# LayerNorm of an image pair: rstd on VectorE and gamma on GpSimd for 17 tiles of each half

## The chip, the core and the metric

The kernel runs on one core of a Trainium2 chip. A core has five engines, each with an instruction queue of its own that it works through in order: TensorE (PE, with its weight loads as PEld), VectorE (DVE), ScalarE (ACT), GpSimd (POOL) and SyncE (SP), which here only issues DMAs. Engines wait for each other through semaphores. The metric is the device time of one execution in microseconds; the profile adds a trace of one execution, in which times are counted from the start of its span.

## The reference

Two layers, on 32 images of 128 channels and 56x56 pixels, all in float32. The first is a depthwise convolution, a LayerNorm over channels and a mixture of experts; the second a coordinate attention and a 3x3 convolution. The change lies in the LayerNorm and what hangs on it:

```python
x = conv_general_dilated(input, dw_kernel, (1, 1), ((3, 3), (3, 3)), feature_group_count=C) + dw_bias
x = transpose(x, (0, 2, 3, 1))
mu = x.mean(-1, keepdims=True)
var = x.var(-1, keepdims=True)
x = (x - mu) / sqrt(var + 1e-06) * ln_gamma + ln_beta
xf = x.reshape(T, C)                       # T = 32*56*56 = 100352 tokens
logits = xf @ Wg + bg                      # 8 experts
topv, topi = top_k(logits, 2)
wts = softmax(topv, axis=-1)
...
return input + x_skip + moe_out            # x_skip is the normalised x
```

## The kernel before

The program runs in stages, one after the other. (1) The depthwise convolution writes its result to DRAM (`y_d`), line 165 and what is around it. (2) The LayerNorm with the gates, lines 194 to 349: the stage of the change. (3) Routing and the experts, lines 352 and on. (4) The combination, attention and the second convolution, with its GpSimd transforms around lines 1022 to 1032.

Stage 2 goes over 16 pairs of images. A pair has 49 tiles of 128 tokens (`TPP`), taken as two halves, the `Unit`s, of 24 and 25 tiles. For each half:

- `centre`: a load of the pair (line 298, SP's queue); for each tile a product on TensorE with a matrix `proj` that subtracts the mean over the channels and gives the 8 logits beside it (line 310); ScalarE copies three tiles at a time to `cen` (line 311), and squares: in the first half tile by tile with a sum (line 315), in the second into `sqs` (line 317).
- `spread`: in the second half VectorE sums the squares (line 322). GpSimd makes the variance (line 323) and `rstd` by a power of -0.5 (line 324), for all tiles of the half in one instruction each.
- `normalise`: VectorE multiplies each tile of `cen` by `rstd` and gamma into the pair's row buffer `pair.row` (called `xn`), line 331, one instruction a tile; then the logits by `rstd` (line 333).

For each pair, `top` finds the two best experts (lines 237 to 252), ScalarE an exponential (line 255), and `gates` makes the weights, writes them into the last columns of the row buffer (lines 261 to 274) and issues the store of the row buffer to `acc_d` (line 276, SP's queue, 3356.5 KB). A row of `xn` has 137 numbers: 128 channels, 8 gates and a mark.

Buffers limit how far engines run ahead: four of `cen` (halves), two of `xn` (pairs), two of the loaded image pair, three of `rstd` and of `var` (halves), eight PSUM tiles of three token tiles each.

The order in which the instructions of each engine stand is settled when the program is built: the framework's scheduler places them by its own estimates of cost, so that instructions of one pair stand between those of another, and adds the semaphore waits. The engines keep to that order when the program runs.

Of the kernel before, what the change touches and what calls it, by code (L numbers as in the profile page):

```python
# [13 lines left out]
ALU = mybir.AluOpType  # L14
# [4 lines left out]
N, C, H, W = 32, 128, 56, 56  # L19
# [5 lines left out]
P = 128  # L25
# [17 lines left out]
def bc(ap, shape):  # L43
    return ap.to_broadcast(shape)
# [3 lines left out]
def moe_conv_then_coordatt_kernel(ctx: ExitStack, tc: tile.TileContext, a: dict, out: bass.AP):  # L48
    nc = tc.nc
# [14 lines left out]
    def load(name, shape, src, eng=None):  # L64
        t = const.tile(list(shape), F32, name=name)
        (eng or nc.sync).dma_start(t, src)
        return t
# [12 lines left out]
    gamma_bc = load("gamma_bc", [P, C], a["ln_gamma"].rearrange("c x -> x c").partition_broadcast(P))  # L80
# [113 lines left out]
    with ExitStack() as st:  # L194
# [6 lines left out]
        halves = ((0, TPP // 2), (TPP // 2, TPP))  # L201
        U = TPP - TPP // 2
        NSQ = TPP // 2
        rank_e = sp.tile([P, E], F32, name="rank_e", bufs=1)
        for e in range(E):
            nc.gpsimd.memset(rank_e[:, e : e + 1], float(E - e))
# [11 lines left out]
        def over_experts(x, n):  # L218
            return bc(x.unsqueeze(2), [P, n, E])
# [60 lines left out]
        class Unit:  # L280
# [12 lines left out]
            def centre(self):  # L293
# [8 lines left out]
                self.var = self.tile(sp, "var")  # L302
                self.alone = 0 if self.h else NSQ
                if self.alone < self.n:
# [21 lines left out]
            def normalise(self):  # L326
                pair = pairs[self.i]
                if self.h == 0:
                    pair.open()
                for j in range(self.n):  # L330
                    nc.vector.scalar_tensor_tensor(pair.row[:, self.j0 + j, 0:C], self.cen[:, j, 0:C],
                                                   self.rstd[:, j : j + 1], gamma_bc, ALU.mult, ALU.mult)
                nc.vector.tensor_tensor(pair.l[:, self.j0 : self.j1, :], self.cen[:, :, C : C + E],
                                        over_experts(self.rstd, self.n), ALU.mult)

        units = [Unit(i, h) for i in range(NPAIR) for h in range(2)]
        for k in range(len(units) + 3):

            pair = pairs[(k - 3) // 2] if k >= 3 else None
# [797 lines left out]
```

## Time and profile before

| what | us |
|---|---|
| median of 6 runs | 4894.09 |
| lowest and highest of the 6 | 4870.55, 4899.64 |
| the profiled execution | 4895.35 |
| its span | 4893.3 |
| stage 2 in it | 627 to 1095 |
| in these 468 us: PE, PEld busy | 364.1, 350.3 |
| DVE busy | 429.5 |
| ACT busy | 289.1 |
| POOL busy | 168.4 |

Over the whole span PE is busy for 74%, DVE 53%, POOL 56%, ACT 30%. The first number of a row of groups is the busy time of the group in us, the next the mean duration of one instruction in ns, and behind the bar stands the idle time of the engine before these instructions, with what ended it. Instructions of one engine overlap a little, so that the step from one to the next can be shorter than a duration.

In stage 2 the store of a pair is issued every 27.47 us (809.87, 837.33, 864.80) and the load of an image pair as often (791.32, 818.80, 846.27).

### The profile page before, as it was taken

How to read it: one execution, taken by the hardware profiler on the slowest of the kernel's cores; microseconds unless marked ns; L12 is line 12 of the kernel's file. 1: busy time of each engine (PE TensorE's matmuls, PEld its weight loads, DVE VectorE, ACT ScalarE, POOL GpSimd, SP SyncE). 2: the span in 40 equal slices, each digit the busy share in tenths (PEclk: the TensorE clock that was granted, in tenths of full speed). 3: DMA queues.
4: the chain of work that ended last, by engine and by line, in shares of the span. 5: the costliest groups of instructions: out<-in, count | busy, mean ns of one | idle time of the engine just before them, and what ended most of it. 6: DMA issues, size and time to landing. Idle time of an engine off the chain costs nothing. (4 is left out here: it accounts for less than half of the span.)

```text
span 4893.3 us, 60979 instructions
## 1 busy us (share of the span) xinstructions
PE 3630.5 (74%) x21765; PEld 2039.8 (42%) x21765; DVE 2585.5 (53%) x5562; ACT 1444.2 (30%) x3123; POOL 2738.3 (56%) x2044
## 2 busy tenths in 40 slices
PE   7998988841486486567557756677775998999999
PEld 4555488741243243233223323233332454545444
DVE  3333359996365267464521211111125888888787
ACT  0000066630232232223223323233341233333323
POOL 5444333331556654464555455655547878788875
PEclk9999998865687788778778977788887999999999
DMA  9999956539611211111111111111115555555552
GB/s 179 188 187 182 159 214 252 232 163 335 195 35 34 49 38 36 35 42 34 48 43 38 43 43 42 45 37 39 42 41 189 165 189 189 163 185 183 190 165 78
DMA packets 678003, 580.90 MB, mean 119 GB/s; under 512 B 405848, under 2 KB 611184, under 8 KB 667248
## 3 DMA queue, kind: packets, MB, share of 16 engines
q1 hardware_dynamic: 411408, 319.81, 22.8%
q10 hardware_dynamic: 222816, 160.70, 12.5%
q0 software_dynamic: 43264, 94.64, 7.2%
q8 instruction: 186, 3.05, 0.3%
q14 instruction: 329, 2.70, 0.2%
HBM read 314.92 MB, written 260.09 MB: 118 GB/s over the span
## 5 line engine op out<-in xcount | busy, mean ns | idle before, releaser
L703 POOL DMA_INDIRECT acc_d<-yo,row x676 | 703.1, 1040 | 756.2 <-issue 474.1
L662 PE MATMUL ph<-fxt,w 128*128 128x512 f32 (+1 forms) x1400 | 753.4, 674 | 401.2 <-ACT ht L663 364.9
L1042 PE MATMUL pc<-v,wk 128*128 128x392 f32 x1920 | 704.9, 509 | 0.4 <-POOL v L1027 0.4
L663 ACT ACTIVATE ht<-ph,bias 128x512 f32<-128x512 f32 (+1 forms) x700 | 473.1, 682 | 719.4 <-remote 334.2
L670 PE MATMUL py<-ht,w 128*128 128x512 f32 (+1 forms) x1400 | 658.8, 615 | 0.0
L641 POOL DMA_INDIRECT xg_r<-acc_d,idx x556 | 534.0, 960 | 197.5 <-issue 153.1
L165 PE MATMUL acc<-xs,band 28*64 28x432 f32 (+1 forms) x11264 | 538.2, 530 | 60.3 <-issue 39.2
L662 PEld LDWEIGHTS ph<-fxt,w 128*128 128x128 f32 x1400 | 276.7, 214 | 723.0 <-ACT ht L663 447.4
L1042 PEld LDWEIGHTS pc<-v,wk 128*128 128x128 f32 x1920 | 348.0, 191 | 308.9 <-issue 105.7
L165 PEld LDWEIGHTS acc<-xs,band 28*64 28x64 f32 x11264 | 308.7, 133 | 289.2 <-issue 184.7
L310 PE MATMUL lnps<-proj,lnyt 128*128 128x136 f32 x1568 | 364.1, 398 | 68.3 <-ACT sq L315 39.0
L670 PEld LDWEIGHTS py<-ht,w 128*128 128x128 f32 x1400 | 270.9, 202 | 287.8 <-issue 285.9
L310 PEld LDWEIGHTS lnps<-proj,lnyt 128*128 128x128 f32 x1568 | 350.3, 315 | 82.7 <-ACT sq L315 48.1
L654 DVE COPY fxt<-pt 128x512 f32<-128x512 f32 (+1 forms) x175 | 119.4, 683 | 439.4 <-remote 184.4
L1052 DVE SCALAR_TENSOR_TENSOR y<-pc,y 128x392 f32<-128x392 f32 x640 | 317.4, 553 | 13.8 <-PE pc L1042 13.8
L697 DVE TENSOR_TENSOR ys<-pb,xg_r 128x512 f32<-128x512 f32 (+2 forms) x147 | 98.4, 671 | 425.3 <-PE pb L679 245.6
L959 POOL TENSOR_TENSOR cxn<-cxn,cx 128x896 f32<-128x896 f32 x112 | 268.0, 2401 | 80.3 <-DMA cxn<-acc_d 34.7
L672 ACT ACTIVATE fyt<-py,b 128x512 f32<-128x512 f32 (+1 forms) x175 | 119.4, 682 | 650.3 <-PE py L670 471.9
L1022 POOL TENSOR_TENSOR d<-pad 128x3248 f32<-128x3248 f32 x32 | 228.0, 7126 | 147.7 <-DVE pad L1014 147.7
L181 DVE TENSOR_TENSOR yt<-acc,m 128x448 f32<-128x448 f32 x256 | 143.8, 619 | 268.0 <-PE acc L165 247.1
L448 PE MATMUL ps_r<-cnt_r,ones 128*128 128x1 f32 x400 | 85.1, 293 | 265.9 <-DVE junk L447 119.9
L641 POOL DMA_INDIRECT xg_f<-acc_d,idx x120 | 115.1, 959 | 225.8 <-DVE thr_r L460 90.1
(244 smaller groups left out, 5258.1 us busy)
## 6 DMA issues: line engine op xcount, KB each, us to landing
acc_d<-xn SPq DMA_DIRECT2D x16, 3356.5 KB
acc_d<-yo ACTq DMA_DIRECT2D x4, 13426.0 KB
lnyt<-y_d SPq DMA_DIRECT2D x16, 3136.0 KB
x<-in_x SPq DMA_DIRECT2D x16, 3136.0 KB
cxn<-acc_d SPq DMA_DIRECT2D x112, 448.0 KB
cx<-acc_d SPq DMA_DIRECT2D x112, 448.0 KB
out<-y ACTq DMA_DIRECT2D x64, 784.0 KB
xt<-in_x SPq DMA_DIRECT2D x64, 392.0 KB
```

The source lines that it names most:

```text
L165: nc.tensor.matmul(acc[r][half * M : (half + 1) * M, :, lo:hi], lhsT=band[rows, t0 + o - least, 1 - par : 1 - par + M], rhs=xs[i][rows, ha ...
L181: nc.vector.tensor_tensor(yts[r][:, :, i - 1 : W : 2], acc[r], common[r], ALU.add)
L310: nc.tensor.matmul(ps[:, j, :], lhsT=yf[:, self.j0 + g + j, :], rhs=proj, start=True, stop=True)
L641: d = nc.gpsimd.indirect_dma_start(out=xg[0:n, k, :], out_offset=None, in_=acc_d[0:T1, :], in_offset=bass.IndirectOffsetOnAxis(ap=idx[0][0 ...
L662: nc.tensor.matmul(ph[:, 0:N_], lhsT=w[0][:, f * P : (f + 1) * P], rhs=xt[:, 0:N_], start=True, stop=True)
L663: nc.scalar.activation(ht[:, f, 0:N_], ph[:, 0:N_], AF.Gelu, bias=w[2][:, f : f + 1])
L670: nc.tensor.matmul(py[:, 0:N_], lhsT=w2[:, f, :], rhs=ht[:, f, 0:N_], start=(f == 0), stop=(f == NF - 1))
L703: d = nc.gpsimd.indirect_dma_start(out=acc_d[:, :], out_offset=bass.IndirectOffsetOnAxis(ap=row[0:n, k : k + 1], axis=0), in_=yo[0:n, k, : ...
L959: nc.gpsimd.tensor_tensor(xn, xn, x2, ALU.add)
L1022: nc.gpsimd.tensor_tensor(d, high, low, ALU.subtract)
L1042: nc.tensor.matmul(m[k], lhsT=wk[k][:, dw, :], rhs=v[:, k, rows, dw : dw + W], start=(dw == 0), stop=(dw == 2))
L1052: nc.vector.scalar_tensor_tensor(r[x], m[k], f, r[y_], ALU.mult, ALU.add)
```

## The change

In `normalise`, 17 of the 24 or 25 tiles of a half are no longer taken one by one. One VectorE instruction multiplies the 17 tiles by `rstd`, spread over the channels, into the row buffer; one GpSimd instruction then multiplies these 17 tiles in the row buffer, in place, by gamma, spread over the tiles. The other 7 or 8 tiles stay as they were.

```diff
         NSQ = TPP // 2
+        NTWO = 17
...
                 if self.h == 0:
                     pair.open()
-                for j in range(self.n):
+                two = pair.row[:, self.j0 : self.j0 + NTWO, 0:C]
+                shape = [P, NTWO, C]
+                nc.vector.tensor_tensor(two, self.cen[:, 0:NTWO, 0:C], bc(self.rstd[:, 0:NTWO].unsqueeze(2), shape), ALU.mult)
+                nc.gpsimd.tensor_tensor(two, two, bc(gamma_bc.unsqueeze(1), shape), ALU.mult)
+                for j in range(NTWO, self.n):
                     nc.vector.scalar_tensor_tensor(pair.row[:, self.j0 + j, 0:C], self.cen[:, j, 0:C],
                                                    self.rstd[:, j : j + 1], gamma_bc, ALU.mult, ALU.mult)
```

`bc` spreads an operand to a shape without copying it. The store of a pair now waits for GpSimd as well as for VectorE. The scheduler places the instructions of stage 2 anew; in the built program the logits of both halves now stand ahead of the multiplications of the first, and both halves of a pair are multiplied close to each other.

## The prediction

> **What bounds the kernel now.** I read the busy time of each engine in stretches of the LayerNorm stage first, then the groups of that stage, then its order of time. The columns of the first view are the stretch in us from the span's start, its length, and for PE, PEld, DVE, ACT and POOL the busy us with the number of instructions; then the granted clock, the share of DMA and GB/s.
>
> ```profile
> 720.00:780.00 60.00, 51.63 (x222) 49.42 (x221) 59.32 (x164) 40.33 (x169) 21.84 (x10) 0.87 0.60 244
> 780.00:840.00 60.00, 51.49 (x217) 48.74 (x217) 59.32 (x171) 40.99 (x175) 25.95 (x9) 0.84 0.58 237
> 840.00:900.00 60.00, 51.53 (x219) 48.91 (x218) 59.28 (x173) 39.17 (x166) 23.88 (x10) 0.83 0.63 258
> ...
> ```
>
> VectorE is busy 59.3 of every 60 us: it sets the pace of this stage, which runs from 627 us to 1095 us. TensorE comes next, and its weight loads (one for each matmul) came back to back at 10.69 us for 48 from 818.85 on, so 98 of them, one pair of images, need about 21.8 us. A pair takes 27.47 us now (the tile reductions on line 322 start at 803.60 and 831.07). ScalarE works 18.5 us of that, GpSimd 11. The groups show what VectorE does and what GpSimd waits for:
>
> ```profile
> L331 DVE SCALAR_TENSOR_TENSOR xn<-cen,rstd,gamma_bc 128x128 f32<-128x128 f32 x784 | 213.9, 344 | 47.3 <-POOL rstd L324 47.3
> ...
> L324 POOL TENSOR_TENSOR rstd<-var,mhalf 128x24 f32<-128x24 f32 (+1 forms) x32 | 139.7, 4364 | 2.7
> ...
> L322 DVE TENSOR_REDUCE var<-sqs 128x25 f32<-128x3200 f32 x16 | 55.7, 3481 | 4.0 <-ACT sqs L317 4.0
> L323 POOL TENSOR_SCALAR var<-var 128x24 f32<-128x24 f32 (+1 forms) x32 | 26.4, 826 | 320.0 <-DVE var L322 169.9 <-ACT sq L315 149.9
> ```
>
> The change takes from the top line and gives to GpSimd, which is idle most of the stage. The question is whether the two engines can work at the same time on such operations. Two places in the order of time answer it, the first just behind the stage, the second in the last one (start, duration, engine, line):
>
> ```profile
> 1095.62 0.57 DVE L248 TENSOR_TENSOR oh<-rank_e,second 128x392 f32<-128x392 f32 x1
> 1095.65 2.88 POOL L723 TENSOR_TENSOR w<-w,ls_bc 128x512 f32<-128x512 f32 x2 [3.46 <-DMA w<-in_W]
> 1096.11 1.27 DVE L252 TENSOR_TENSOR later<-later,second 128x49 f32<-128x49 f32 x1
> 1097.30 1.30 DVE L262 TENSOR_TENSOR w<-m,one_t 128x49 f32<-128x49 f32 x1
> 1098.52 0.23 DVE L270 SCALAR_TENSOR_TENSOR xn<-later,all_e 128x49 f32<-128x49 f32 x1
> ```
> ```profile
> 3744.88 7.05 POOL L1022 TENSOR_TENSOR d<-pad 128x3248 f32<-128x3248 f32 x1 [7.17 <-DVE pad L1014]
> ...
> 3748.55 0.56 DVE L983 TENSOR_REDUCE cs<-cpa 128x56 f32<-128x392 f32 x1
> 3749.03 2.98 DVE L990 TENSOR_TENSOR rs<-rs,wq 128x56 f32<-128x56 f32 x1
> 3751.89 3.07 POOL L1026 TENSOR_TENSOR t<-pad,t 128x1624 f32<-128x1624 f32 x1
> ```
>
> Line 723 is the very form that the change adds: GpSimd multiplies a tile in place by a row that is repeated. While its two instructions ran, line 252 took 1.27 us and line 262 took 1.30 us; both take 0.20 and 0.21 us elsewhere. In the second place GpSimd's line 1022 ran from 3744.88 to 3751.93: the reduction on line 983 (one input, from PSUM) passed in its usual 0.56 us, but line 990, with both inputs in SBUF, has 56 elements and took 2.98 us, until 3752.01, when line 1022 was through. So a VectorE operation with two SBUF inputs stands still while GpSimd streams a two-input operation, and VectorE, being in order, stands with it.
>
> **What is removed.** 17 of line 331's instructions in each of 32 half pairs, 544 in all. In a run of them the step is 0.262 us (21 of them lasted 5.58 us, the last one 0.344). So 17 x 0.262 = 4.45 us for a half, 142.5 us in all, all of it on VectorE, which sets the end of the stage.
>
> **What VectorE gets.** One TENSOR_TENSOR of 17x128 = 2176 elements a half. Its price from two rows: 392 elements take 0.555 us, 3136 elements on line 1013 at least 3.40 us, so 1.037 ns an element and 0.555 + 1784 x 0.001037 = 2.40 us; following operations start 0.08 us before the end (line 267 to 268: 0.48 us apart, 0.55 long). 2.33 us, times 32 is 74.4 us. Net relief of VectorE: 142.5 - 74.4 = 68 us.
>
> **What GpSimd gets.** The nearest row is line 723, at least 1.26 us for 512 elements; line 1022 took 7.05 us for 3248, so 2.12 ns an element, and 2176 elements take 1.26 + 1664 x 0.00212 = 4.78 us. The cheapest two-input row, line 141 (3.17 us for 1792), would give 3.85; the dearest, line 1031 (1.92 for 812), 5.1. I take 4.78, as the form is line 723's. GpSimd then has 11 + 9.6 = 21 us of work in a pair: not a bound.
>
> **What it costs VectorE.** Line 252 lost 1.07 us and line 262 lost 1.09 to operations of 1.26 us, so all but some 0.18 us. For 4.78 us that is 4.60, in 32 halves 147 us, if VectorE always has a two-input operation next. The bounds: nothing at all, if the new operation behaved like GpSimd's power on line 324, beside which two-input operations ran at their usual 0.34 and 0.55 us (it has 25 elements and computes for 4.3 us); and all of it, 4.78 x 32 = 153. The form decides for 4.60.
>
> From this goes what VectorE can do meanwhile: operations with one input. Its order in the built program decides. Behind the new multiplication of the first half come seven of the old operations, then, in 8 of the 16 pairs, after one more small operation, the reduction of line 322 (3.48 us). GpSimd seems not to get in between such a run: its 24-element line 323, usually 0.21 us, took 1.83 us at 815.26, until the run of line 331 and line 333 had ended at 817.03. So in these 8 pairs I let the pass start with the reduction, and 3.4 us are covered: 27 us. In the other 8 pairs, and for second halves, only the short reductions of the top-2 search (0.56 us) can cover something: about 5 us. Blocked: 147 - 27 - 5 = 115 us. In the first 60 us of the stage VectorE still has about 6 us of idle time, of which I let 4 go. **Sum: 115 - 68 - 4 = +43 us.**
>
> The Trainium skill ("SBUF — State Buffer", section "Who interferes with whom") has a rule that speaks against this change: a VectorE instruction with two SBUF inputs and a GpSimd instruction that reads SBUF exclude each other, and the one issued second waits for the whole instruction. Lines 252, 262 and 990 agree; line 324 (4.31 us, nothing blocked) does not fit its letter. By the rule the second pass would block for the whole 4.78 us, 6 us more in all than by the row.
>
> **Waits that move.** The store of a pair (line 276) now also waits for GpSimd. In the built order it is issued behind the next pair's first multiplication, nearly a period after the second pass of its own pair became ready, so that is hidden; were it not, the next pair but one would wait for its row buffer (two of them) and, on SP's queue, the next image load. GpSimd's queue holds the variance and the power of later halves behind the new passes: up to 5 us each, and what needs them on VectorE stands more than 10 us later. VectorE's order now takes both halves of a pair together, so ScalarE gets its buffer of centred tiles later; it idles 6.9 + 1.9 us a pair today, which covers it. All three would show as waits on VectorE; I cost them at nothing. Later stages keep their order but for a moved count on TensorE and small setup steps.
>
> **The time.** The profiled execution took 4895.35 us (span 4893.3), 1.3 above the median of 4894.09. 4895.35 + 43 = **4938 us**.
>
> **Rivals.**
> 1. *Nothing is covered* (slower): GpSimd gets in at the first boundary between two instructions, as it did between lines 248 and 252, before VectorE reaches the reduction. Then 147 - 68 = +79, 4974 us. At the dearest price (5.1 us) it is +89, 4985. Against it stands line 323's wait. Chance 0.22.
> 2. *Much is covered* (no change): the passes land on reductions wherever there are any: 16 x 3.48 and 16 x 0.56 = 65 us covered, 147 - 65 - 68 - 4 = +10, 4905 us; or the pass has line 141's price: 3.7 x 32 = 118, less 32, 68 and 4, +14. Chance 0.10. From about 0.3% (15 us) a change can be told from none.
> 3. *The engines don't exclude each other here* (faster): VectorE then needs 27.47 - 4.25 = 23.2 us a pair, still above TensorE's 21.8; the gain is 68 us less some that the first pairs, bound by TensorE, can't use: 4832 us. Line 324 speaks for it, lines 252, 262, 990 against. It decides if less than 68 of the 147 us block. Chance 0.09.
> 4. *A new wait* (row buffer or rstd) adds to the forecast, some 2 us a pair: 4970. Chance 0.06.
>
> The forecast has 0.53; its own range is 4918 to 4962 (the price between 4.3 and 5.1 us, cover between 15 and 45 us). With rival 1 above and the half of rival 2 that is slower the range is 4900 to 4985. Slower: 0.53 + 0.22 + 0.06 + 0.01 = 0.82; same 0.09; faster 0.09.
>
> **What would show it.** In the profile after: GpSimd's new group at about 4.8 us (longer where it waits to get in), VectorE's new one at 2.4 us when not blocked; single operations of lines 331, 244 or 248 of 4 to 5 us instead of 0.34 to 0.57; a pair at 29 to 31 us; VectorE busy all the time, by recorded durations that contain the block. Wrong it would be with VectorE's operations at their usual lengths (rival 3, pair at 23 us), or with VectorE idle for a DMA or for rstd (rival 4).

## The result and the profile after

The changed kernel takes 4943.45 us (median of 20 runs, 4915.72 to 4962.83), the kernel before 4892.34 us beside it (46 runs). The ratio is 1.0106, with a 95% interval of 1.0092 to 1.0119: slower by about 51 us.

The profiled execution of the changed kernel took 4926.79 us (span 4924.7), only 31 us above the one of before. One execution of each is a weak comparison, since the other stages differ too: from the end of stage 2 to the first product of the second convolution (line 1042 before, 1047 after) it is 2655.8 us before and 2639.7 us after, in code that the change does not touch. So the length of stage 2 itself, from its first product to the first count of the routing behind it, is the measure used from here on. The two views below are the busy time of the engines in just that stretch, first before, then after. Columns: stretch, length, then PE, PEld, DVE, ACT and POOL busy with the number of instructions, granted clock, DMA share, GB/s.

```profile
627.30:1102.50 475.20, 366.15 (x1577) 352.21 (x1577) 436.97 (x1250) 289.30 (x1201) 171.26 (x84) 0.83 0.53 213
```
```profile
623.10:1151.80 528.70, 360.64 (x1568) 349.50 (x1568) 493.57 (x736) 280.82 (x1201) 352.18 (x114) 0.79 0.47 189
```

The stage grew by 53.5 us, which accounts for the 51 us of the medians. VectorE runs 514 instructions fewer and is busy 56.6 us longer; it is idle 35.1 us, before 38.2. GpSimd's busy time doubles. In the three stretches of 60 us that were shown of before, after:

```profile
720.00:780.00 60.00, 47.71 (x210) 46.47 (x210) 59.49 (x86) 34.62 (x150) 43.40 (x13) 0.86 0.59 242
780.00:840.00 60.00, 44.81 (x193) 42.96 (x194) 59.45 (x91) 34.73 (x150) 44.79 (x12) 0.83 0.54 220
840.00:900.00 60.00, 41.45 (x179) 39.79 (x179) 59.42 (x84) 32.93 (x145) 42.28 (x12) 0.74 0.47 190
```

VectorE is still busy for 59.4 of every 60 us and still sets the pace; TensorE now does less in the same time. Three periods between stores lie between 792.45 and 886.23 us and between 886.23 and 980.02: 31.26 us a pair against 27.47.

The groups of the stage after show where VectorE's time went. The line numbers after the change are 5 higher behind `normalise` and 1 higher ahead of it: 333 is the new VectorE multiplication, 334 GpSimd's pass, 336 the tiles taken one by one, 323 the reduction.

```profile
L334 POOL TENSOR_TENSOR xn<-xn,gamma_bc 128x2176 f32<-128x2176 f32 x32 | 144.0, 4501 | 32.6 <-DVE xn L333 32.2
L336 DVE SCALAR_TENSOR_TENSOR xn<-cen,rstd,gamma_bc 128x128 f32<-128x128 f32 x240 | 139.2, 642 | 0.0
...
L333 DVE TENSOR_TENSOR xn<-cen,rstd 128x2176 f32<-128x2176 f32 x32 | 77.3, 2415 | 50.2 <-POOL rstd L325 50.2
L323 DVE TENSOR_REDUCE var<-sqs 128x25 f32<-128x3200 f32 x16 | 55.4, 3465 | 0.0
...
L245 DVE TENSOR_TENSOR gt<-lgs,m 128x392 f32<-128x392 f32 x32 | 32.7, 1021 | 0.8
L251 DVE SCALAR_TENSOR_TENSOR lgs<-oh,lgs 128x392 f32<-128x392 f32 x16 | 30.5, 1904 | 0.5
L249 DVE TENSOR_TENSOR oh<-rank_e,later 128x392 f32<-128x392 f32 x16 | 21.9, 1370 | 0.5
```

The tiles taken one by one last 642 ns on average instead of 344, and three operations of the top-2 search, which the change does not touch, have means 1.8 to 3.4 times their usual 0.57 us. The reduction keeps its 3.5 us, and line 333 takes the 2.4 us that it was reckoned at. The order of time tells when it happens (start, duration, engine, line), first VectorE's, then GpSimd's:

```profile
808.91 2.42 DVE L333 TENSOR_TENSOR xn<-cen,rstd 128x2176 f32<-128x2176 f32 x1
811.25 6.11 DVE L336 SCALAR_TENSOR_TENSOR xn<-cen,rstd,gamma_bc 128x128 f32<-128x128 f32 x7
817.27 0.56 DVE L269 TENSOR_TENSOR gt<-oh,w 128x392 f32<-128x392 f32 x1
817.75 3.48 DVE L323 TENSOR_REDUCE var<-sqs 128x25 f32<-128x3200 f32 x1
821.15 0.55 DVE L270 TENSOR_TENSOR xn<-xn,gt 128x392 f32<-128x392 f32 x1
...
828.97 0.57 DVE L249 TENSOR_TENSOR oh<-rank_e,later 128x392 f32<-128x392 f32 x1
829.57 4.89 DVE L251 SCALAR_TENSOR_TENSOR lgs<-oh,lgs 128x392 f32<-128x392 f32 x1
```
```profile
811.41 4.49 POOL L334 TENSOR_TENSOR xn<-xn,gamma_bc 128x2176 f32<-128x2176 f32 x1 [1.17 <-DVE xn L333]
821.32 3.89 POOL L324 TENSOR_SCALAR var<-var 128x25 f32<-128x25 f32 x1 [5.42 <-DVE var L323]
825.29 4.31 POOL L325 TENSOR_TENSOR rstd<-var,mhalf 128x25 f32<-128x25 f32 x1
829.57 4.47 POOL L334 TENSOR_TENSOR xn<-xn,gamma_bc 128x2176 f32<-128x2176 f32 x1
```

GpSimd's pass starts at 811.41, 0.16 us into a run of seven single operations, and ends at 815.90. The seven take 6.11 us instead of 1.92 (six steps of 0.262 and a last one of 0.344). The pass of the second half starts at 829.57 together with line 251, which takes 4.89 us instead of 0.57. The 3.48 us of the reduction, beside which GpSimd could stream for nothing, come at 817.75, when the first pass is over.

### The profile page after: what moved, and what is told of

Its sections match the earlier page's. It is cut to its first block, busy times and chain, and to the rows that moved or that the text cites. A ratio compares the mean times of both kernels' runs of the same rounds, so it can differ in the third digit from the quotient of the medians.

```text
span 4924.7 us, 60480 instructions
## 1 busy us (share of the span) xinstructions
PE 3628.1 (74%) x21765; PEld 2040.6 (41%) x21765; DVE 2645.5 (54%) x5050; ACT 1438.1 (29%) x3123; POOL 2940.6 (60%) x2076
## 5 line engine op out<-in xcount | busy, mean ns | idle before, releaser
L708 POOL DMA_INDIRECT acc_d<-yo,row x676 | 704.2, 1042 | 737.4 <-issue 450.3
L964 POOL TENSOR_TENSOR cxn<-cxn,cx 128x896 f32<-128x896 f32 x112 | 279.0, 2499 | 80.1 <-DMA cxn<-acc_d 44.6
```

Source lines behind the costliest of these rows:

```text
L708: d = nc.gpsimd.indirect_dma_start(out=acc_d[:, :], out_offset=bass.IndirectOffsetOnAxis(ap=row[0:n, k : k + 1], axis=0), in_=yo[0:n, k, : ...
L964: nc.gpsimd.tensor_tensor(xn, xn, x2, ALU.add)
```

## The experiments

Twelve runs were made, four at a time, each four beside the kernel before on one chip: nine new kernels, the change once more, and two of the nine a second time. On the chip of the first and the last four everything ran faster than in the first measurement (before: 4339 and 4335 us), on that of the second four not (before: 4910 us). The difference lies behind stage 2: from its end to the first product of the second convolution every kernel took 2640 to 2667 us in the first measurement and on the chip of the second four, and 2090 to 2102 us on the other. Why stays open. Stage 2 itself agrees between the chips for each of the three kernels that were profiled on both: 528.7 and 528.5 us for the change, 507.1 and 507.0, 423.5 and 423.3 for experiments 5 and 8. So stage lengths are compared across all runs, with the 475.2 us of the one profile of the kernel before, and medians only within one set of four.

**1. The multiplication by gamma on VectorE.** It keeps the new order and the two passes, and takes GpSimd out.

```diff
-                nc.gpsimd.tensor_tensor(two, two, bc(gamma_bc.unsqueeze(1), shape), ALU.mult)
+                nc.vector.tensor_tensor(two, two, bc(gamma_bc.unsqueeze(1), shape), ALU.mult)
```

> The gamma pass goes from GpSimd to VectorE, all else as in the change. Theory (GpSimd's streaming pass holds VectorE): no VectorE operation of the stage is longer than usual; a half costs 2 x 2.33 = 4.66 us where 17 single operations cost 4.45, so +7 us on the stage against before (475 us from the first LayerNorm matmul to the first threshold count; 529 after the change): 475 to 485, and the whole within 0.3% of before, 4885 to 4907. Rival (the new order of the stage, or waits for row buffers and rstd, cost the time): the stage stays above 510 and the whole above 4930.

Measured: 4356.33 us against 4338.98, ratio 1.0033 (1.0011 to 1.0055); the stage took 490.1 us. No VectorE operation of the stage was drawn out to 4 us. The stage is some 5 us longer than expected: of the 14.9 us above the kernel before, about 7 are the two passes themselves (two of 2.33 us for 17 steps of 0.262, 0.21 us more in each of 32 halves), and about 8 are idle time of VectorE (46.1 us in the stage against 38.2). The new order is the likely reason for these 8; no run shows it apart. What follows: VectorE does both passes itself 38.6 us cheaper than it does one of them with GpSimd's help.

**2. No multiplication by gamma, and 3. a GpSimd pass that only writes.**

```diff
-                nc.gpsimd.tensor_tensor(two, two, bc(gamma_bc.unsqueeze(1), shape), ALU.mult)
```
```diff
-                nc.gpsimd.tensor_tensor(two, two, bc(gamma_bc.unsqueeze(1), shape), ALU.mult)
+                nc.gpsimd.memset(two, 1.0)
```

> The multiplication of the 17 tiles by gamma is left out, so this measures the relief alone. Theory: 544 single operations at 0.262 us less 32 long ones at 2.33, 68 us less than before, and perhaps 9 more by the new order: stage 398 to 410 us, whole 4815 to 4830. Rival (TensorE at 21.8 us a pair, a buffer or a store bounds the stage as soon as VectorE is faster): stage above 430, whole above 4845, with VectorE idle.

> GpSimd's pass is a memset of the same 17 tiles, which reads nothing (the tiles are overwritten by 1). Same queue, same semaphores. Theory (the shared thing is the reading of SBUF): VectorE at its usual lengths, stage as with gamma left out, within 6 us. Rival 1 (any streaming GpSimd instruction stops VectorE): a memset of 3584 elements took 3.09 us, so 1.9 us for 2176, times 32 is 60 us: stage 460 to 470. Rival 2 (it is the waits for GpSimd): stage longer with VectorE idle.

Measured: 4268.69 us, ratio 0.9844 (0.9825 to 0.9863), stage 414.4 us; and 4280.15 us, ratio 0.9871 (0.9852 to 0.9890), stage 414.5 us. The stage without the pass is 4 us above the expected range; VectorE is idle for 48.5 us of it, before for 38.2. Without the pass VectorE is busy for 365.9 us of the stage, 71 less than before and 127.6 less than with it. The groups of the kernel without the pass:

```profile
L333 DVE TENSOR_TENSOR xn<-cen,rstd 128x2176 f32<-128x2176 f32 x32 | 77.4, 2417 | 50.4 <-POOL rstd L325 50.4
L335 DVE SCALAR_TENSOR_TENSOR xn<-cen,rstd,gamma_bc 128x128 f32<-128x128 f32 x240 | 66.9, 344 | 0.0
...
L245 DVE TENSOR_TENSOR gt<-lgs,m 128x392 f32<-128x392 f32 x32 | 18.1, 567 | 0.8
...
L249 DVE TENSOR_TENSOR oh<-rank_e,later 128x392 f32<-128x392 f32 x16 | 9.1, 567 | 0.5
L251 DVE SCALAR_TENSOR_TENSOR lgs<-oh,lgs 128x392 f32<-128x392 f32 x16 | 9.1, 567 | 0.5
```

The difference to the groups of the changed kernel is the block, line by line: 72.3 us on the tiles taken one by one, 14.6 on line 245, 21.4 on line 251, 12.8 on line 249, and 7.2 on the small lines 263 and 266, together 128.3 us, or 4.0 us for each of the 32 passes.

The pass that only writes streams as many numbers to the same place at the same point of the order, and blocks nothing; GpSimd's and VectorE's order of time in that kernel:

```profile
809.27 1.92 POOL L334 MEMSET xn<- 128x2176 f32 x1 [0.97 <-DVE xn L333]
```
```profile
809.13 1.92 DVE L336 SCALAR_TENSOR_TENSOR xn<-cen,rstd,gamma_bc 128x128 f32<-128x128 f32 x7
```

Both run at their full pace side by side. So it is not enough that GpSimd writes the same tiles at the same point; the passes that block, here and in experiment 4, also read them.

**4. A GpSimd pass with one input.**

```diff
-                nc.gpsimd.tensor_tensor(two, two, bc(gamma_bc.unsqueeze(1), shape), ALU.mult)
+                nc.gpsimd.tensor_scalar(two, two, 1.0, None, ALU.mult)
```

> GpSimd's pass is a multiplication by the number 1 in place: one input from SBUF (gamma is left out for the 17 tiles). Theory (a GpSimd instruction that reads SBUF stops VectorE's two-input operations for its length): a copy of 1792 elements took 1.85 us, so some 2.2 us for 2176, 2.0 of it blocking, 64 us in all: stage 462 to 475. Rival (only a GpSimd instruction with two inputs blocks): stage as with gamma left out, 398 to 410. If it waits for VectorE as the variance on GpSimd did (1.8 to 4.3 us before it got in) its own duration will be much longer than 2.2 us.

Measured: 4421.14 us, ratio 1.0203 (1.0176 to 1.0229), stage 559.3 us. This expectation was wrong by some 90 us: with one input the pass is slower, not faster. GpSimd's group and one run of single operations on VectorE:

```profile
L334 POOL TENSOR_SCALAR xn<-xn 128x2176 f32<-128x2176 f32 x32 | 186.3, 5822 | 26.2 <-DVE xn L333 25.8
```
```profile
817.24 7.16 DVE L336 SCALAR_TENSOR_TENSOR xn<-cen,rstd,gamma_bc 128x128 f32<-128x128 f32 x7
```

The seven take 7.16 us, 5.24 above their 1.92, beside a pass of 5.76 us. So one input is enough for the block, and a longer pass blocks longer.

**5. The pass starts only behind the single tiles**, so that the reduction follows it.

```diff
-                nc.gpsimd.tensor_tensor(two, two, bc(gamma_bc.unsqueeze(1), shape), ALU.mult)
                 for j in range(NTWO, self.n):
-                    nc.vector.scalar_tensor_tensor(...
+                    last = nc.vector.scalar_tensor_tensor(...
                                                    self.rstd[:, j : j + 1], gamma_bc, ALU.mult, ALU.mult)
+                late = nc.gpsimd.tensor_tensor(two, two, bc(gamma_bc.unsqueeze(1), shape), ALU.mult)
+                after(late.ins, last.ins, "starts behind the tiles that are taken one by one")
```

> The gamma pass of each half waits for the last of the 7 or 8 tiles that are taken one by one; all else as in the change, and VectorE's order is the same. Theory (the cover was missed because GpSimd's pass gets in after one single operation): in the 8 pairs where the reduction of 3.48 us stands one small operation behind the seven, the pass now begins with the reduction, which it does not stop, so 8 x 3.4 = 27 us less than the change: stage about 502 us instead of 529, and the seven at their usual 1.92 us. Rival (the reduction is held as well, or the pass gets in elsewhere): stage 520 to 535.

Measured: 4955.29 us against 4910.27, ratio 1.0114 (1.0060 to 1.0168, four runs), stage 507.1 us. The median alone could not tell this from the change, the stage could: 21.6 us shorter. VectorE's order and GpSimd's pass:

```profile
814.13 1.92 DVE L335 SCALAR_TENSOR_TENSOR xn<-cen,rstd,gamma_bc 128x128 f32<-128x128 f32 x7
815.97 0.56 DVE L269 TENSOR_TENSOR gt<-oh,w 128x392 f32<-128x392 f32 x1
816.45 3.48 DVE L323 TENSOR_REDUCE var<-sqs 128x25 f32<-128x3200 f32 x1
819.84 1.43 DVE L270 TENSOR_TENSOR xn<-xn,gt 128x392 f32<-128x392 f32 x1
```
```profile
816.13 4.71 POOL L337 TENSOR_TENSOR xn<-xn,gamma_bc 128x2176 f32<-128x2176 f32 x1 [3.02 <-DVE xn L335]
```

The seven are back at 1.92 us, the reduction runs through the pass in its 3.48 us, and only 0.87 us of the block are left, on line 270. That is the cover of the prediction, and here it had to be ordered. It came about for seven passes, each with 0.85 to 0.97 us of block left, where eight were expected. Six others, at other places in the order, began 3.4 to 3.8 us before they stopped anything and lasted 7.7 to 8.2 us.

**6. Eight tiles instead of 17** (`NTWO = 8`).

> 8 tiles instead of 17. Theory (cost goes with the length of GpSimd's pass): relief 8 x 0.262 - 1.13 = 0.97 us a half, 31 in all; the pass has 1024 elements and, between 1.26 us for 512 and 4.47 for 2176, takes 2.25 us, of which 2.07 block, 66 us less 5 covered: net +30, stage about 505 us. Rival (a fixed price for each pass, by semaphores and the new order): stage 520 or more. Rival 2 (order alone, as with both passes on VectorE): about 490.

Measured: 4948.33 us, ratio 1.0083 (1.0051 to 1.0115), stage 504.8 us. Eight tiles cost 29.6 us, 17 cost 53.5: a smaller share loses less, and neither size gains.

**7. The kernel before, with the passes added and nothing taken away:** 17 tiles of each half are multiplied once more, in place, by a row of ones on GpSimd.

```diff
+    ones_bc = const.tile([P, C], F32, name="ones_bc")
+    nc.gpsimd.memset(ones_bc, 1.0)
...
+                two = pair.row[:, self.j0 : self.j0 + 17, 0:C]
+                nc.gpsimd.tensor_tensor(two, two, bc(ones_bc.unsqueeze(1), [P, 17, C]), ALU.mult)
```

> The kernel before, with all tiles one by one on VectorE, plus a pass on GpSimd in place by a row of ones over the same 17 tiles: the block without the relief. Theory: 4.29 us a half less some 10 covered, 127 us: stage about 600 us against 475, whole run 2.5 to 3% above before. Rival (the change's cost lies in the new order or in waits, not in the pass): less than 60 us.

Measured: 5036.62 us, ratio 1.0273 (1.0222 to 1.0323), stage 603.5 us, 128.3 above the kernel before:

```profile
629.50:1233.00 603.50, 368.96 (x1577) 352.90 (x1577) 566.29 (x1251) 290.97 (x1201) 366.67 (x116) 0.77 0.41 168
```

VectorE has the work of before and is busy 129.3 us longer. The price of the passes, 4.0 us each, comes out the same in another order of work. The moment at which a pass gets in does not. Here the pass begins late in a run of 23 single operations, on line 333 of this kernel; GpSimd's order of time and VectorE's:

```profile
803.68 6.59 POOL L336 TENSOR_TENSOR xn<-xn,ones_bc 128x2176 f32<-128x2176 f32 x1 [5.92 <-DVE xn L333]
```
```profile
799.32 6.12 DVE L333 SCALAR_TENSOR_TENSOR xn<-cen,rstd,gamma_bc 128x128 f32<-128x128 f32 x23
...
805.75 0.24 DVE L272 SCALAR_TENSOR_TENSOR xn<-later,all_e 128x49 f32<-128x49 f32 x1
805.86 4.47 DVE L264 TENSOR_TENSOR w<-m,one_t 128x49 f32<-128x49 f32 x1
```

The run keeps its usual 6.12 us. The pass stops nothing until line 264, 2.2 us after its own start, and lasts 6.59 us instead of 4.5. So it goes with 28 of the 32 passes of this kernel (6.57 to 6.62 us).

**8 and 12. ScalarE in GpSimd's place:** ScalarE scales 12 tiles of a half by `rstd`, tile by tile, and VectorE multiplies them by gamma in one operation. The second run is the same kernel on the chip of the last four.

```diff
-        NTWO = 17
+        NTWO = 12
...
-                nc.vector.tensor_tensor(two, self.cen[:, 0:NTWO, 0:C], bc(self.rstd[:, 0:NTWO].unsqueeze(2), shape), ALU.mult)
-                nc.gpsimd.tensor_tensor(two, two, bc(gamma_bc.unsqueeze(1), shape), ALU.mult)
+                for j in range(NTWO):
+                    nc.scalar.activation(pair.row[:, self.j0 + j, 0:C], self.cen[:, j, 0:C], AF.Copy, scale=self.rstd[:, j : j + 1])
+                nc.vector.tensor_tensor(two, two, bc(gamma_bc.unsqueeze(1), shape), ALU.mult)
```

> A way without GpSimd: rstd is applied by ScalarE, tile by tile, for 12 tiles of a half, and gamma by one VectorE operation of 1536 elements for them; the rest one by one as before. VectorE saves 12 x 0.262 - 1.66 = 1.48 us a half, 47 in all. ScalarE gets 24 instructions a pair of 0.2 to 0.28 us, 5 to 7 us on top of 18.5, and VectorE then needs 24.5 a pair. Theory: stage 430 to 450 us, whole 0.5 to 1% faster than before. Rival (ScalarE, in order, waits for rstd and then hands over its copies late): stage 475 or more.

> rstd on ScalarE for 12 tiles, gamma on VectorE, once more with more rounds: its stage was 423.5 us, 51.7 less than before. Theory: 0.8 to 1.1% faster than before.

Measured: 4867.48 us against 4910.27, ratio 0.9914 (0.9881 to 0.9946); and 4292.64 against 4334.67, ratio 0.9904 (0.9873 to 0.9934). The stage took 423.5 and 423.3 us, less than expected. This version is 0.9 to 1.0% faster than the kernel before. Its stage, ScalarE's new group and VectorE's new operation:

```profile
623.70:1047.20 423.50, 363.84 (x1572) 350.32 (x1572) 384.20 (x898) 373.90 (x1585) 182.72 (x83) 0.90 0.60 238
```
```profile
L334 ACT ACTIVATE xn<-cen,rstd 128x128 f32<-128x128 f32 x384 | 140.3, 521 | 4.5 <-DVE lgs L238 4.5
```
```profile
811.89 1.75 DVE L335 TENSOR_TENSOR xn<-xn,gamma_bc 128x1536 f32<-128x1536 f32 x1
```

ScalarE's instructions last 521 ns on average, twice what was expected, but they overlap (384 of them make 140.3 us of busy time). They do not hold VectorE up: its single tiles take 342 ns there, its work falls by 52.8 us, and the stage gets shorter by 51.7.

**9. The pass cut into 17 operations of one tile each, 10. the change once more, 11. the late pass once more**, all three beside each other.

```diff
-                nc.gpsimd.tensor_tensor(two, two, bc(gamma_bc.unsqueeze(1), shape), ALU.mult)
+                for j in range(NTWO):
+                    nc.gpsimd.tensor_tensor(two[:, j, :], two[:, j, :], gamma_bc, ALU.mult)
```

> The gamma pass as 17 GpSimd instructions of one tile (128 elements) each, in the same place; VectorE's order is that of the change. The 24-element variance waited up to 4.3 us behind VectorE's operations and stopped none of them, while the pass of 2176 elements got in after one operation: does the size of an instruction decide? Theory A (an instruction of any size gets in at the next boundary): 17 x (0.44 - 0.18) = 4.4 us blocked a half as before, stage 515 to 545 us. Theory B (short instructions wait for a gap and stop nobody): stage below 470, single GpSimd instructions of 1 us and more, and GpSimd late.

> The change once more, beside its variants on the same chip: 1.0 to 1.2% above before; stage 525 to 532 us.

> The pass that waits for the single tiles, once more: its stage was 507 us, 21.6 less than the change, but its time, with 4 runs, did not show it. Theory: 0.55 to 0.75% above before, 20 us below the change beside it. Rival (what the stage gains is lost later): as the change.

Measured, against 4334.67 us: the change 4389.15 us, ratio 1.0125 (1.0099 to 1.0151), stage 528.5; the late pass 4370.57 us, ratio 1.0081 (1.0055 to 1.0108), stage 507.0, so it gives back 18.6 us of the medians and 21.5 of the stage; the cut pass 4371.59 us, ratio 1.0091 (1.0060 to 1.0122), stage 512.1. The change and the late pass came out about 0.05% above the ranges expected of them. The cut pass falls between the two theories. GpSimd's group, one run of VectorE beside it, and two of the waits of the stage (us in total, times, longest):

```profile
L335 POOL TENSOR_TENSOR xn<-xn,gamma_bc 128x128 f32<-128x128 f32 x544 | 311.7, 609 | 5.5 <-DVE xn L333 5.1
```
```profile
815.75 3.18 DVE L337 SCALAR_TENSOR_TENSOR xn<-cen,rstd,gamma_bc 128x128 f32<-128x128 f32 x7
```
```profile
ACT cen L312 <- DVE xn L337: 133.7, 24, 16.1
...
DVE lgs L339 <- POOL rstd L325: 30.7, 13, 3.7
```

Seven single operations take 3.18 us instead of 6.11: the engines now take turns (between 816.1 and 818.7 each starts one operation about every 0.45 us), and VectorE is busy only 433.0 us of the stage, 60.6 less than with the whole pass. But GpSimd needs 468 of the 512 us, and VectorE waits 30.7 us for `rstd`, which stands behind the small operations on GpSimd's queue; it is idle for 79.1 us of the stage in all, with the whole pass for 35.1. The block got smaller and a late GpSimd took its place.

## Why the prediction came true, step by step

- **VectorE sets the pace, before and after:** true. It stays busy for 59.4 of 60 us, and the stage's 53.5 us are 56.6 of busy time less 3.1 of idle time.
- **The relief of 68 us:** 71 measured (437.0 to 365.9 without the pass). The new multiplication takes 2.415 us, predicted 2.40.
- **VectorE stands still while GpSimd streams a two-input operation:** true, and the main point. The added passes alone make the kernel before 128.3 us longer in stage 2; a pass that only writes costs nothing in the stage (414.5 us against 414.4). Rival 3, which lived on line 324's power blocking nobody, falls with it.
- **The price of a pass, 4.78 us, and 4.60 of it blocked:** too dear. The pass takes 4.47 to 4.50 us and blocks 4.2 to 4.3 (6.11 less 1.92; 4.89 less 0.57; 4.86 less 0.57 on line 249 of the next pair). At 4.29, 32 of them are 137 us where the prediction had 147: 10 us less.
- **The cover of 32 us:** this step failed, as the prediction put it: "in these 8 pairs I let the pass start with the reduction". It rested on "GpSimd seems not to get in between such a run", read from a 24-element operation that had to wait 1.83 us. In the changed kernel the large pass of a first half starts with the run of single tiles (at 811.41, 0.16 us into it), stops the second of them, and is over when the reduction starts. Of 137 us 128 were paid: 9 were covered, 23 fewer than predicted. The reading itself was not wrong everywhere: in experiment 7 a pass of the same size that begins late in such a run waits for its end. But the changed kernel's passes start at the head of the run, and the 24-element operation, which began 4.1 us into a run of 21, did not show that case. What decides when a pass gets in stays open. That the size of the cover was reckoned well is shown by experiments 5 and 11: with the pass held back, 21.5 us return.
- **Idle time:** 3.1 us less, predicted 4.
- **Waits that move:** true for VectorE. In the steady part of the stage it waits neither for the row buffer nor for `rstd` (rival 4 falls). ScalarE does wait for its buffer of centred tiles (122.7 us in the stage, behind line 336), which costs nothing as long as VectorE is the bound.

With the measured terms the sum is 137 − 9 − 71 − 3 = +54 us, against +43 predicted and 53.5 measured. The forecast of 4938 us came within 6 us of the median because a cover too large by 23 us met a price too dear by 10 and a relief too small by 3; that they met so closely is luck. In its mechanism rival 1 was nearer, as GpSimd does get in at the first boundary in this kernel; its +79 is too much by the same price and relief, and by the 9 us that were covered after all.

The rule that the prediction weighed against its rows, in the Trainium skill, "SBUF — State Buffer", section "Who interferes with whom", also says that a VectorE instruction with two SBUF inputs does not contend with a GpSimd instruction which only writes, and that a reduction never contends. Experiment 3 (414.5 us of stage against 414.4) and the reduction's 3.48 us inside the late pass agree. Its sentence that the other engine waits for the whole instruction holds in the changed kernel to within 0.2 to 0.3 us of 4.5. That the one issued second is the one to wait, as the prediction puts the rule, does not fit experiment 7: there the pass began at 803.68, and VectorE operations that started up to 2.1 us later went ahead of it.

## What to carry to other kernels

Work taken off a busy VectorE and given to GpSimd as a reading pass comes back as a block, as long as VectorE's stream is of operations with two SBUF inputs: here 71 us of relief were paid with 128 us of block. Before such a move, look in the order of time for an ordinary VectorE operation that lasts as long as the GpSimd operation beside it, and reckon with no cover unless the order forces one. ScalarE, busy for 289.3 of the 475.2 us, took the multiplication by `rstd` for 12 tiles of a half without that price.

## What the runs showed of the hardware that was not expected

- A GpSimd operation with one input on 2176 numbers, in place, takes 5.8 us, longer than the two-input multiplication by a row (4.5 us); filling the same numbers takes 1.92 us.
- When a GpSimd pass gets in between VectorE's operations varies. In the changed kernel a pass that starts with a run of single tiles stops the second of them; in experiment 7 the same-sized pass waited 2.2 us through the rest of such a run, and in experiment 6 ten of the 32 passes lasted 4.7 to 5.5 us instead of 2.2. The 25-element variance of line 324 can last 3.89 or 4.35 us instead of 0.21 to 0.4 without any VectorE operation being drawn out by it. What they wait for stays open.
- The 25-element power of line 325 works for 4.3 us and draws no VectorE operation out: beside the one that ran from 825.29 to 829.60 eight single operations took 2.16 us. Being busy on GpSimd is not what blocks.
